# A deformable convolution that gathers a pixel with three differences: one multiply-add and one scaling a tap, two summing transposes

## The chip, the cores and the metric

The kernel runs on one core of a Trainium2 chip. The metric is the device time of one execution in microseconds (us). Engines are named as the profile names them: PE is TensorE (PEld its weight loads), DVE is VectorE, ACT is ScalarE, POOL is GpSimd, SP is SyncE, whose queue issues most DMAs. All data are 32-bit floats.

## What is computed

Two layers of a "metaformer" over x of shape (4, 128, 128, 128): four images, 128 channels, 128 rows, 128 columns. The part that matters here is the token mixer of layer 0, a deformable 3x3 convolution on the channel-normalised image. An ordinary 3x3 convolution gives 18 offsets a pixel, a (dy, dx) for each of nine taps. Each tap reads the image at its shifted, fractional place, as a weighted sum of the four pixels around it, and the nine samples are multiplied by nine 128x128 matrices and summed:

```python
offset = _offset_conv(x, w_off)                      # 18 channels
py = base_y + dy ; px = base_x + dx                  # of 9 taps
y0 = jnp.floor(py); x0 = jnp.floor(px)
wy1 = py - y0; wy0 = 1.0 - wy1
wx1 = px - x0; wx0 = 1.0 - wx1
sampled = (corner(y0, x0, wy0 * wx0) + corner(y0, x1, wy0 * wx1)
         + corner(y1, x0, wy1 * wx0) + corner(y1, x1, wy1 * wx1))
return jnp.einsum('bckhw,ock->bohw', sampled, w_conv.reshape(O, C, K * K))
```

A corner outside the image counts as zero. Behind the mixer come a mixture of eight experts for each token, a second mixer (an FFT pair that reduces to a channel product with a mirrored image) and a layer of 64 experts for selected tokens.

## The kernel before, in words

**Stages.** For each image a *table* is built in device memory (`tabs`, class `Image`, line 260): the normalised image with a border, where an entry (i, j) holds the 128 channels of the pixels (i-1, j-1) and (i, j-1), 1 KB; rows have `TC` = 130 entries. Two entries next to each other are the four corners of a sample, so a gather reads 2 KB at index `ylo * TC + xlo`. The image's `index` and `weight` tiles hold that index and the four products wy * wx for each pixel and tap. The first image's table is built ahead of the main loop, those of images 1 to 3 inside it, while the image before is sampled. The last image's period also holds the middle part of the 64 experts for images 0 to 2; a tail after the loop does the rest.

**Building a table.** `table_of` starts a `block` (line 507) for each 8 image rows. Its two halves (`half`, line 527) transpose four rows each to pixels by channels (`tr`), copy them to `raw`, compute mean and variance on VectorE, and write the normalised rows into `ent`. One DMA a block writes each row twice, as the lower pixel of one entry row and the upper one of the next; `ent[:, 0]` is a copy of the last row of the block before (`tails`). `padding` and `offsets` turn the same rows into the offset convolution, and `positions` with `axis_of` (lines 623 and 597) turn offsets into indices and weights for 16 rows.

**The main loop.** 4 images x 32 groups of four rows x 4 rows x 3 chunks of three taps: 1536 chunks of class `Chunk` (line 731), one to a *slot*. What is done for a chunk:

- `gather` (737): three indirect DMAs on POOL fill the chunk's buffer `g` [128 pixels, 3 taps, 4 corners, 128 channels]. There are `AHEAD` = 7 buffers; the gather for chunk n+7 is issued at the end of slot n and waits for chunk n's buffer.
- `weighted` (750), one slot before the sum: VectorE multiplies the corners by their weights, in one instruction for three taps (128x1536) if it is the first chunk of its row, and for two taps (128x1024) else. The weights come from `spread`, a tile in PSUM that `Group.weights` (693) fills by ScalarE copies. For the other chunks `weighted_too` (758) lets ScalarE scale the third tap, corner by corner.
- `summed` (766): TensorE transposes the four corners of each tap to channels by pixels, all into the same place of a PSUM bank `trg`, which adds them up: 12 transposes.
- `moved` (780), two slots later: ScalarE copies `trg` to `sT`. After each fourth chunk `convolved` multiplies by the tap matrices into the PSUM tile `sums`, and after the ninth tap `mixed` carries the group through the rest of the layer (experts `pe`, mirrored mixer, gate).

**What sets the order.** Engines run their instructions strictly in program order (`InOrder`), and waits are semaphores that the framework places. The order is written by hand: in each slot the loop at the end calls the steps of the chunks in flight, then `turns.steps()` resumes the jobs (generators) of the other work. A job that yields `FILL` waits until PSUM banks are to be had: `fills` (147) counts the banks taken in the last two slots against `BANKS` = 6. `turns.hop` is 1 before the main loop and 2 in it.

Of the kernel before, what the change touches and what calls it, by code (L numbers as in the profile page):

```python
# [51 lines left out]
P = 128  # L52
# [5 lines left out]
HID = 512  # L58
# [12 lines left out]
TC = P + 2  # L71
# [11 lines left out]
BANKS = 6  # L83
# [103 lines left out]
def metaformer_kernel(  # L187
# [50 lines left out]
    with ExitStack() as main:  # L238
# [19 lines left out]
        spread = p_s.tile([P, 2, 4, 4 * TAPS], F32, name="spread")  # L258

        class Image:  # L260


            def __init__(self, b):
                self.b = b
                self.table = tabs.tile([TW * TC, 2 * P], F32, name=f"table{b}", tag="table")
                self.grid = self.table.rearrange("(i j) e -> i j e", j=TC)
# [8 lines left out]
                self.offsets = self.placed = self.known = 0  # L275
# [4 lines left out]
            def room(self, q):  # L280
                return pw.tile(
                    [P, CB, TAPS, 4],
                    F32,
                    name=f"weight{self.b}_{q}",
                    tag="weight",
                    bufs=3 * P // CB // 2,
                )
# [7 lines left out]
            def border(self):  # L295

                eng.sync.dma_start(
                    out=self.grid[0:P, 0 : TC : TC - 1, :],
                    in_=zeros.unsqueeze(1).to_broadcast([P, 2, 2 * P]),
                )  # L300
                eng.sync.dma_start(
                    out=self.grid[P:TW, 0 : TC : TC - 1, :],
                    in_=zeros[0:1].unsqueeze(1).to_broadcast([1, 2, 2 * P]),
                )
# [46 lines left out]
        for base in (0, -P):  # L351
# [6 lines left out]
                pattern=[[1, P]],  # L358
                channel_multiplier=1,
# [75 lines left out]
        def padding(t, h, row, read, padded):  # L435

            yield FILL
            tr = transposes(row, 4)
            read.append(h)
            yield turns.hop  # L440
            eng.scalar.copy(pads[(2 * t + h) % 4][:, :, 1 : P + 1], tr)
            padded.append(h)

        def offsets(im, t, padded):
# [8 lines left out]
            for k in range(3):  # L453
                for h in range(2):
# [6 lines left out]
                    )  # L461
            yield turns.hop
# [31 lines left out]
        def again(im, t):  # L494
# [4 lines left out]
                in_=im.grid[t * RB : (t + 1) * RB, 1 : P + 1, P : 2 * P].rearrange("i x c -> x i c"),  # L499
# [3 lines left out]
            for h in range(2):  # L503
                turns.start(padding(t, h, lambda i, h=h: xc[:, 4 * h + i, :], [], padded))
            yield from offsets(im, t, padded)

        def block(im, t):

            while im.continued < t - 1 or im.sent < t - 1 or im.read < 2 * t:
                yield 1  # L510
            last = t == P // RB

            ent = pa.tile([P, RB + 1, P], F32, name=f"ent{im.b}_{t}", tag="ent")
            if t == 0:
                eng.vector.memset(ent[:, 0, :], 0.0)
            if last:
                eng.vector.memset(ent[:, 1, :], 0.0)
            else:
# [5 lines left out]
            im.tails[t] = ent[:, RB, :]  # L524
            halves, padded = [], []

            def half(h):
                yield FILL
                tr = transposes(lambda i: xc[:, 4 * h + i, :], 4)
                im.read += 1  # L530
                yield turns.hop
                raw = pa.tile([P, 4, P], F32, name="raw", tag="raw")
# [9 lines left out]
                yield 1  # L542
                if turns.hop == 1:

                    r, nb = rn
                    for i in range(1, 4, 2):
                        eng.vector.tensor_scalar(
                            ent[:, 1 + 4 * h + i, :],
# [7 lines left out]
                    normalise(  # L556
                        lambda i: raw[:, 2 * i, :], lambda i: ent[:, 1 + 4 * h + 2 * i, :], 2, even
                    )
                else:
                    normalise(  # L560
                        lambda i: raw[:, i, :], lambda i: ent[:, 1 + 4 * h + i, :], 4, rn
                    )
                yield 1
                if t < im.direct:
                    yield from padding(t, h, lambda i: ent[:, 1 + 4 * h + i, :], halves, padded)
                else:
                    halves.append(h)
# [8 lines left out]
            while im.normed < t:  # L576
                yield 1
            if t > 0:
                eng.scalar.copy(ent[:, 0, :], im.tails.pop(t - 1))
                im.continued = t  # L580
            while not last and len(halves) < 2:
                yield 1
            im.normed = t + 1
            n = 1 if last else RB
            i0 = t * RB
            yield 1
            pairs = ent[:, 0:2, :].rearrange("p i c -> p (i c)").unsqueeze(1)
            pairs = bass.AP(
                pairs.tensor, pairs.offset, [pairs.ap[0], [P, n], [1, 2 * P]]
            )  # L590
            eng.sync.dma_start(
                out=im.grid[i0 : i0 + n, 1 : P + 1, :].rearrange("i x e -> x i e"), in_=pairs
            )
            im.sent = t + 1
            im.left -= 1

        def axis_of(pos, which):
# [5 lines left out]
            w = pt.tile([P, 2, CB, TAPS], F32, name=f"w{which}", tag=f"w{which}")  # L603
# [13 lines left out]
            eng.vector.tensor_tensor(w[:, 1], pos, lo, ALU.subtract)  # L617
            yield 0
            eng.vector.tensor_scalar(w[:, 0], w[:, 1], -1.0, 1.0, ALU.mult, ALU.add)
            yield 1  # L620
            return lo, w

        def positions(im, q):
# [21 lines left out]
            ylo, wy = yield from axis_of(py, "y")  # L645
            xlo, wx = yield from axis_of(px, "x")
            eng.vector.scalar_tensor_tensor(xlo, ylo, float(TC), xlo, ALU.mult, ALU.add)
            yield 0
            eng.vector.tensor_copy(im.index[:, rows, :], xlo)
            im.weight[q] = im.rooms.pop(q, None) or im.room(q)  # L650
# [1061 lines left out]
```

## Time and profile before

| | before |
|---|---|
| median of 3 runs | 7367.58 us (7365.69 to 7368.79) |
| the profiled execution: its time / its span | 7358.05 us / 7356.1 us |
| mean granted TensorE clock | 0.896 |
| first gather / last gather issued at | 135.3 / 7123.6 us |
| first / last copy of `trg` to `sT` starts at | 146.5 / 7141.5 us |
| DMA queues, share of 16 engines' span: gathers q0, others q1 | 55.0% + 12.1% |
| moved by DMA | 1524.69 MB, 207 GB/s |

A page of the profile gives busy times of each engine, and then groups of like instructions: line, engine, operation, out<-in by tile names, count, then busy time and mean duration of one in ns, then idle time of the engine just before them and what ended most of it. "remote" is a semaphore event that the profile can't put down to an instruction, and "issue" is time in which the engine waited for nothing shown. All instructions that the wrapper `InOrder` issues have line 101, so groups are told apart by tile names. In a timeline the columns are start in us, duration in us, engine, operation, tiles, and in brackets the idle time before.

By image, the main loop's busy time a chunk is 3.75 to 3.81 us on PE, 2.93 to 3.04 on DVE, 2.19 to 2.38 on ACT and 2.85 to 2.86 on POOL, of 4.52 to 4.63 us.

### The profile page before, as it was taken

How to read it: one execution, taken by the hardware profiler on the slowest of the kernel's cores; microseconds unless marked ns; L12 is line 12 of the kernel's file. 1: busy time of each engine (PE TensorE's matmuls, PEld its weight loads, DVE VectorE, ACT ScalarE, POOL GpSimd, SP SyncE). 2: the span in 40 equal slices, each digit the busy share in tenths (PEclk: the TensorE clock that was granted, in tenths of full speed). 3: DMA queues.
4: the chain of work that ended last, by engine and by line, in shares of the span. 5: the costliest groups of instructions: out<-in, count | busy, mean ns of one | idle time of the engine just before them, and what ended most of it. 6: DMA issues, size and time to landing. Idle time of an engine off the chain costs nothing. (4 is left out here: it accounts for less than half of the span.)

```text
span 7356.1 us, 103037 instructions
## 1 busy us (share of the span) xinstructions
PE 6006.3 (82%) x31271; PEld 3981.9 (54%) x31271; DVE 4789.5 (65%) x16100; ACT 3707.7 (50%) x9999; POOL 4432.3 (60%) x4691
## 2 busy tenths in 40 slices
PE   5788888887888888887888888888877788788885
PEld 3455555555555555555555555555555555555553
DVE  5466666676667666666667666667667665566663
ACT  4345555554555555554455555555444444444452
POOL 1666666666666666666666666666666665666641
PEclk7888999998898998998899999898898999899897
DMA  6666666666666666666666666666666677677777
GB/s 204 191 200 212 204 207 210 202 194 188 197 201 203 205 206 200 204 193 186 193 209 200 207 202 201 198 199 210 186 189 181 201 250 238 180 247 237 246 236 273
DMA packets 578917, 1524.69 MB, mean 207 GB/s; under 512 B 86424, under 2 KB 225408, under 8 KB 578368
## 3 DMA queue, kind: packets, MB, share of 16 engines
q0 software_dynamic: 369664, 1210.35, 55.0%
q1 hardware_dynamic: 206400, 299.36, 12.1%
q10 hardware_dynamic: 2304, 8.39, 0.3%
q8 instruction: 254, 4.16, 0.2%
q14 instruction: 295, 2.42, 0.1%
HBM read 1380.92 MB, written 136.85 MB: 206 GB/s over the span
## 5 line engine op out<-in xcount | busy, mean ns | idle before, releaser
L101 POOL DMA_INDIRECT g<-table,index x4608 | 4377.4, 950 | 2710.4 <-issue 1190.9
L101 PEld LDWEIGHTS trg<-ident,g 128*128 128x128 f32 x18432 | 2300.2, 150 | 1501.3 <-issue 1288.2
L101 PE MATMUL trg<-ident,g 128*128 128x128 f32 x18432 | 2575.2, 288 | 562.9 <-issue 465.9
L101 DVE SCALAR_TENSOR_TENSOR x<-pe,scaled,x 128x128 f32<-128x128 f32 x4048 | 1379.7, 341 | 1432.5 <-remote 644.6
L101 DVE TENSOR_TENSOR g<-g,spread 128x1024 f32<-128x1024 f32 (+1 forms) x1536 | 2129.1, 1387 | 202.4 <-DMA g<-table,index 90.0
L101 ACT COPY sT<-trg 128x384 f32<-128x384 f32 x1536 | 720.5, 472 | 2742.1 <-remote 1187.4
L101 PE MATMUL sums<-sT,wconv_sb 128*128 128x512 f32 x2304 | 1326.6, 658 | 53.1 <-issue 50.9
L101 ACT ACTIVATE g<-g,weight 128x128 f32<-128x128 f32 x4096 | 1306.3, 394 | 1.9 <-DMA g<-table,index 1.7
L101 PE MATMUL pe<-ew_sb,x1T 128*128 128x512 f32 x2048 | 1163.6, 649 | 147.0 <-issue 88.6
L101 PEld LDWEIGHTS sums<-sT,wconv_sb 128*128 128x128 f32 x2304 | 435.1, 208 | 518.9 <-issue 516.5
L101 PEld LDWEIGHTS pe<-ew_sb,x1T 128*128 128x128 f32 x2048 | 343.7, 205 | 261.1 <-issue 182.3
L101 ACT ACT_TABLE_LOAD x270 | 346.4, 1283 | 23.5 <-DVE nmax L101 9.8
L101 PE MATMUL sums<-xg,ident 128*128 128x512 f32 x256 | 163.8, 726 | 125.8 <-ACT x1T L101 96.8
L101 DVE TENSOR_TENSOR x<-ps,x 128x512 f32<-128x512 f32 x128 | 88.1, 688 | 264.5 <-remote 119.6
L101 PE MATMUL po<-pad,woff_sb 128*64 128x512 f32 x768 | 216.1, 645 | 17.8 <-issue 11.0
L101 DVE TENSOR_TENSOR x<-x,pe 128x512 f32<-128x512 f32 x128 | 87.0, 679 | 217.8 <-remote 130.4
L101 PE MATMUL pl<-rw_sb,x1T 128*128 128x8 f32 x1024 | 143.9, 256 | 98.2 <-issue 88.7
L101 ACT ACTIVATE tn<-x,d_nb,d_rs 128x128 f32<-128x128 f32 x512 | 211.2, 487 | 5.5 <-DVE x L101 2.6
L101 ACT ACTIVATE xn<-x,c_nb,c_rs 128x128 f32<-128x128 f32 x512 | 210.6, 485 | 4.7 <-issue 1.8
L101 PEld LDWEIGHTS pl<-rw_sb,x1T 128*128 128x128 f32 x1024 | 147.3, 213 | 98.5 <-issue 88.6
L101 ACT ACTIVATE ent<-raw,a_nb,a_rs 128x128 f32<-128x128 f32 x448 | 185.0, 485 | 7.6 <-remote 3.8
L101 PE MATMUL pe<-eb_sb,gT 32*128 32x512 f32 x256 | 169.4, 740 | 20.0 <-issue 14.6
(227 smaller groups left out, 5130.9 us busy)
## 6 DMA issues: line engine op xcount, KB each, us to landing
g<-table,index POOLq DMA_INDIRECT x4608
table<-ent SPq DMA_DIRECT2D x64, 1024.0 KB
xc<-in_x SPq DMA_DIRECT2D x64, 512.0 KB
w<-x_d SPq DMA_DIRECT2D x64, 512.0 KB
xg<-in_x SPq DMA_DIRECT2D x124, 256.0 KB
x_d<-x SPq DMA_DIRECT2D x124, 256.0 KB
out<-w SPq DMA_DIRECT2D x48, 512.0 KB
w<-in_weight SPq DMA_DIRECT2D x40, 512.0 KB
```

The source lines that it names most:

```text
L101: return self.tc.keep_in_program_order(issue(*args, **kwargs))
```

## The change

An entry of the table grows from 1 KB to 2 KB and becomes a pixel with three differences, so that one entry holds all that a sample needs. With A the pixel above left, the sample is (A + wy * B) + wx * (C + wy * D), where B is the step downwards, C the step sideways and D the step downwards of C. An entry is laid out [A, C, B, D].

- The table: `TC` goes, rows have `TW` = 129 entries of 4 x 128 floats. A half block (`STEP` = 4 rows) is stored by itself. The step sideways is a matmul with the matrix `step` (-1 on the diagonal, +1 beside it; it mixes partitions, which are pixels) into a PSUM bank `beside`, copied by ScalarE; the step downwards is one subtraction of 128x1024 a half block, on GpSimd ahead of the main loop and on VectorE in it, after a copy of the last row of the half block before. The left border of each row gets its entries by small DMAs (`edge`), one more for each row of the image. `ent` has three buffers.
- Positions: the weights kept are wy and wx alone, computed straight into `weight`; the complements and the four products go, as do `spread` and `Group.weights`. `BANKS` becomes 7.
- The chunk: `down` (VectorE, three multiply-adds of 128x256, both tensors in SBUF, the weight a pointer to a column in SBUF) two slots before the sum; `beside` (ScalarE, three scalings of 128x128) one slot before; `summed` does two transposes a tap instead of four. The loop starts one slot earlier for it.
- Buffers of the 64 experts' weights move: one of `OWN` = 9 tiles of the end is made from two halves in two pools.

The core of the diff:

```diff
-                self.table = tabs.tile([TW * TC, 2 * P], F32, name=f"table{b}", tag="table")
-                self.grid = self.table.rearrange("(i j) e -> i j e", j=TC)
+                self.table = tabs.tile([TW * TW, 4 * P], F32, name=f"table{b}", tag="table")
+                self.grid = self.table.rearrange("(i j) e -> i j e", j=TW)
...
+                yield FILL
+                beside = bank([P, STEP, P], "beside")
+                eng.tensor.matmul(beside, lhsT=step, rhs=new[0], start=True, stop=True)
+                yield turns.hop
+                eng.scalar.copy(new[1], beside)
...
+                free = eng.gpsimd if turns.hop == 1 else eng.vector
+                if u == 0:
+                    free.memset(ent[:, 0:2, :], 0.0)
+                else:
+                    free.tensor_copy(ent[:, 0:2, :], im.tails.pop(u - 1))
...
+                free.tensor_tensor(
+                    of[:, :, half_of:], here[:, :, half_of:], of[:, :, 0:half_of], ALU.subtract
+                )
+                yield 1
+                stored(u, ent, STEP)
...
+            def stored(u, ent, n):
+
+                i0 = u * STEP
+                eng.sync.dma_start(
+                    out=im.grid[i0 : i0 + n, 1 : P + 1, :].rearrange("i x e -> x i e"),
+                    in_=ent[:, 0 : 4 * n].rearrange("p (i s) c -> p i (s c)", s=4),
+                )
+                for i in range(n):
+                    eng.sync.dma_start(
+                        out=im.edge(i0 + i, 1, 1),
+                        in_=ent[0:1, 4 * i : 4 * i + 4 : 2, :],
+                    )
+                im.sent = u + 1
...
-            for s in range(4):
-                if s % 2 == 0:
-                    yield 1
-                eng.vector.tensor_tensor(
-                    im.weight[q][:, :, :, s], wy[:, s % 2], wx[:, s // 2], ALU.mult
-                )
...
-            def weighted(self):
-                n = 2 if self.shared else 3
-                gf = self.g[:, 0:n].rearrange("p k s c -> p (k s) c")
-                w = self.row.group.w[:, self.row.s, 4 * self.k0 : 4 * (self.k0 + n)]
-                eng.vector.tensor_tensor(
-                    gf, gf, w.unsqueeze(2).to_broadcast(list(gf.shape)), ALU.mult
-                )
...
+            def down(self):
+
+                for i in range(3):
+                    eng.vector.scalar_tensor_tensor(
+                        self.g[:, i, 0:2, :],
+                        self.g[:, i, 2:4, :],
+                        self.weight(i, 0),
+                        self.g[:, i, 0:2, :],
+                        ALU.mult,
+                        ALU.add,
+                    )
+
+            def beside(self):
+
+                for i in range(3):
                     eng.scalar.activation(
-                        g[:, v, :], g[:, v, :], AF.Copy, scale=w[:, y % CB, self.k0 + 2, v : v + 1]
+                        self.g[:, i, 1, :], self.g[:, i, 1, :], AF.Copy, scale=self.weight(i, 1)
                     )
...
-                    for v in range(4):
+                    for v in range(2):
...
-            if n + 1 < total:
-                chunk[n + 1].weighted()
+            if n + 2 < total:
+                chunk[n + 2].down()
...
-            if n >= 0 and n + 3 < total and (n + 3) % 12 == 0:
-                chunk[n + 3].row.group.weights((n + 3) // 12 % 2)
-            if n + 1 < total and chunk[n + 1].shared:
-                chunk[n + 1].weighted_too()
+            if 0 <= n + 1 < total:
+                chunk[n + 1].beside()
```

## The prediction

> **What bounds the kernel now.** I read the page's busy shares first, then the tile `trg` with those who wait for it, then the costliest groups, and last GpSimd's timeline.
>
> ```profile
> PE 6006.3 (82%) x31271; PEld 3981.9 (54%) x31271; DVE 4789.5 (65%) x16100; ACT 3707.7 (50%) x9999; POOL 4432.3 (60%) x4691
> ```
>
> TensorE is the busiest. The view of tile `trg`, the PSUM tile of the summing transposes, says who stands behind it:
>
> ```profile
> L101 ACT COPY sT<-trg x1536: 452/479/509, 146.5 to 7141.5; 128x384 f32<-128x384 f32 x192
> ...
> who waited for it (us, times):
>   ACT sT L101: 597.7, 204
>   POOL g L101: 501.1, 250
>   DVE x L101: 321.0, 107
> ```
>
> Three things: the loop over 1536 chunks (three taps of one image row) runs from 146.5 to 7141.5 us, 6995 us or 4.554 us a chunk; 146.5 us lie before it and 214.6 behind. ScalarE, VectorE and GpSimd wait for these transposes, so TensorE sets the pace. And GpSimd's wait is for buffers, not for work. How far behind it stands is told by a stretch in which its buffers are free, and one in which they run out:
>
> ```profile
> 166.78 0.94 POOL L101 DMA_INDIRECT g<-table,index  x1 [0.30 <-issue]
> 168.03 0.95 POOL L101 DMA_INDIRECT g<-table,index  x1 [0.30 <-issue]
> 173.64 0.95 POOL L101 DMA_INDIRECT g<-table,index  x1 [4.66 <-remote]
> 174.89 0.95 POOL L101 DMA_INDIRECT g<-table,index  x1 [0.30 <-issue]
> ```
>
> Free-running gathers start 1.25 us apart (0.95 of work, 0.30 of issue; from 149.24 to 168.03 there are 15 steps in 18.79 us, 1.253 each). A chunk has three: 3.758 us. The loop therefore has a second floor at 1536 x 3.758 = 5772 us, and the difference of 0.797 us a chunk is what GpSimd now waits.
>
> **The change, part by part.**
>
> ```profile
> L101 PE MATMUL trg<-ident,g 128*128 128x128 f32 x18432 | 2575.2, 288 | 562.9 <-issue 465.9 <-ACT sT L101 33.6 <-DVE g L101 26.9
> L101 PE MATMUL sums<-sT,wconv_sb 128*128 128x512 f32 x2304 | 1326.6, 658 | 53.1 <-issue 50.9 <-ACT sT L101 0.2
> L101 DVE SCALAR_TENSOR_TENSOR x<-pe,scaled,x 128x128 f32<-128x128 f32 x4048 | 1379.7, 341 | 1432.5 <-remote 644.6 <-PE pe L101 293.8 <-PE trg L101 263.8
> L101 ACT ACTIVATE g<-g,weight 128x128 f32<-128x128 f32 x4096 | 1306.3, 394 | 1.9 <-DMA g<-table,index 1.7
> L101 DVE TENSOR_TENSOR g<-g,spread 128x1024 f32<-128x1024 f32 x1024 | 1237.9, 1209 | 171.1 <-ACT spread L101 81.2 <-DMA g<-table,index 63.0 <-issue 12.9
> L101 DVE TENSOR_TENSOR g<-g,spread 128x1536 f32<-128x1536 f32 x512 | 891.3, 1742 | 31.4 <-DMA g<-table,index 27.0 <-issue 2.5 <-PE trg L101 1.9
> ```
>
> *TensorE.* Half of 18432 transposes go: 9216 x 2575.2/18432 = 0.1397 us, 1288 us or 0.838 a chunk, on the pacing path. The new `beside` matmul (128 of them, two passes each like every f32 matmul here) costs 2 x 1326.6/2304 = 1.15 us; 96 fall into the loop: 111 us, 0.072 a chunk. If every other TensorE time and wait stays, the pace is 4.554 - 0.838 + 0.072 = 3.788. A TensorE with less to do may be granted less clock: it had 0.92 in 500 to 1500 us, where it was busy 853 of 1000, and 0.75 at the end, where it was busy 118 of 206. Its busy time would fall from 3.76 to 3.00 a chunk; at 0.80 instead of 0.90 that is 3.38, still under the floor of GpSimd. No charge.
>
> *VectorE.* Out: 2129 us of products, 128 weight products of 0.423 (54), 64 small scalings (15). In: 4608 multiply-adds of 128x256. No such row exists. Below: the two products give 143 ns plus 1.041 an element, 409 ns. Above: the 128x128 multiply-add with a pointer took 341 where that line gives 276, so 65 more, 474. I take 442, the middle: 2037 us. 96 subtractions of 128x1024 at 1.209 and 93 copies of 128x256, at most 0.41 each: 154 us at most. Net about zero, 3.1 us a chunk, under both floors.
>
> *ScalarE.* 512 more scalings at 1306.3/4096 = 0.319 (163), 128 evacuations of `beside` at 0.584 (75, the row of the `raw` copy); 272 copies of spread weights (53) and 64 tail copies (20) go. 165 us more, 2.5 us a chunk: hidden behind GpSimd's 3.76; uncovered it would cost 0.11 a chunk.
>
> *Gathers.* As many, of 2 KB as before. The buffer is needed one slot earlier (`down` at n+2), five slots after it came free instead of six: five slots of 4 us against three issues and a landing. The DMA queues were busy 67% of the span; at 4.07 a chunk that is 75%, and the doubled table (68 MB more on 1525) makes it 78%. No charge.
>
> *A new hold-up.* `spread`, the second operand of the old products, lies in PSUM; both tensor operands of the new multiply-adds lie in SBUF. The trace has a few such instructions in the loop, and they delay gathers:
>
> ```profile
> 251.69 0.44 DVE L101 TENSOR_TENSOR off<-z 128x288 f32<-128x288 f32 x1
> 251.84 1.11 POOL L101 DMA_INDIRECT g<-table,index  x1 [0.30 <-issue]
> ...
> 253.07 0.46 DVE L101 TENSOR_TENSOR off<-off,z 128x288 f32<-128x288 f32 x1 [0.74 <-issue]
> 253.25 1.10 POOL L101 DMA_INDIRECT g<-table,index  x1 [0.30 <-issue]
> ...
> 5655.28 0.69 DVE L101 TENSOR_TENSOR same<-same,val 128x512 f32<-128x512 f32 x1
> 5655.37 1.42 POOL L101 DMA_INDIRECT g<-table,index  x1 [0.30 <-issue]
> ```
>
> Each gather that began inside such an instruction is longer by that instruction's remaining time less about 0.13 us: at 251.84, 0.29 remained and it took 0.16 more; at 5655.37, 0.60 and 0.47. The products with `spread`, in flight during 2533 gathers, leave them at 0.95. With 442 ns a hit costs on average (0.442 - 0.13)^2/(2 x 0.442) = 0.11, with a second one overlapping its end some 0.15; three in 3.9 us are hit by about a third of the gathers: 0.047 a gather, 0.14 a chunk (bounds: nothing; and 0.31 a gather if every one begins just after a multiply-add). The 96 subtractions add 0.01. GpSimd's pace becomes 3.91.
>
> The Trainium skill, "SBUF — State Buffer", section "Who interferes with whom", says that a VectorE instruction with two SBUF inputs and a GpSimd instruction that reads SBUF exclude each other, the later one blocked until the earlier has finished. The trace agrees for the gathers, but not the other way: `off` instructions that began 190 to 770 ns into a gather took 0.44 to 0.47, like the others. By the rule each gather would need 0.95 + 0.30 + 0.44 = 1.69 us, and the total would be about 8,200; an estimate that I set aside for the rows.
>
> *Before the loop.* The first image's table is built before any gather. GpSimd now subtracts there: 456 ns at 128x128 and 725 at 128x256 (its own additions near the end) extend to 2.34 us at 128x1024, with a copy about 3 us, 32 times: 96 us of some 120. The table writes double to 34 MB; the queues were 63% busy in these 135 us. SyncE issues four small edge DMAs more per half block, 0.5 us each by the row of the border's small DMAs. All are under the stage's time but several near it: +20 us (bounds 0 and 45). Behind the loop nothing that counts moves.
>
> *Sum.* The two paces, 3.79 and 3.91, are now so close that each waits for the other. Of the 0.797 that GpSimd waits I leave a fifth, 0.16 (bounds 0 and two fifths): a choice. 4.07 x 1536 = 6252; with 166.5 before and 214.6 behind, 6633. The profiled execution took 7358.05 for a span of 7356.1, 2 more; the median of the runs, 7367.58, is 0.13% over it: 6640.
>
> **The rivals.**
>
> *GpSimd's floor alone* (0.14): few hits, buffers swallow the rest; 3.80 a chunk, 5837 + 381 = 6220. For it: seven chunks of gathers ahead. Against: the shown hold-ups.
>
> *VectorE becomes the pace* (0.13): in program order the multiply-adds wait for gathers, and the sums of the experts `x<-pe` stand behind them. Its 3.1 us plus the 1.13 a chunk for which `x<-pe` now waits (894.7 remote, 389.8 `pe`, 310.4 `trg`, 147.2 `tr`) are 4.25: 6530 + 381 = 6910. Against: that wait is for TensorE, which has less to do.
>
> *Every gather meets a multiply-add* (0.15, slower): if VectorE runs dry, each multiply-add starts when its own gather lands, at a fixed point of GpSimd's rhythm; where that is just ahead of the next gather's start, all pay 0.31: 4608 x 1.565 = 7211 + 381 = 7590. It decides from 0.26 a gather, where the loop takes its present 6995. Against: the phase would have to hold, and VectorE is busy three quarters of the time.
>
> *The transposes were not what paces* (0.03): about 7360. For it: TensorE idles 1350 us, much of it for nothing shown.
>
> **How the numbers follow.** My forecast, 6350 to 6900, has 0.52 plus 0.03 at its edges, 0.55. The range 6200 to 7150 holds it, most of the first rival and the second; its top is 0.10 a gather of hold-up with two fifths of the wait, 4.38 x 1536 + 395 = 7123. Faster 0.55 + 0.14 + 0.13 = 0.82; within 0.2%, about what a measurement of this kernel can tell from no change, 0.03; slower 0.15.
>
> **What would show it.** Gathers with a mean near 1.00 instead of 0.95, their idle time nearly all 0.30 of issue; `trg` 9216 times near 0.14; multiply-adds between 0.41 and 0.47; first `sT` near 166; TensorE busy 72%, at a lower clock. I am wrong if gathers last 1.2 us or more, if VectorE's multiply-adds show waits for gathers as its largest idle time, or if TensorE's busy time falls and its idle time takes the same amount.

## The result, and the profile after

| | before | after |
|---|---|---|
| median | 7367.58 us (7363.04 to 7370.72, 5 runs) | 7407.54 us (7401.98 to 7412.89, 5 runs) |
| after / before | | 1.0054, 95% interval 1.0040 to 1.0069 |
| span of the profiled execution | 7356.1 us | 7405.5 us |
| first gather | 135.3 us | 203.3 us |
| main loop, first to last start of `sT` | 6995.0 us | 6975.1 us |
| mean granted TensorE clock | 0.896 | 0.830 |

Half a per cent slower, where 6640 us were forecast. Three parts of the changed kernel's profile answer to those shown of before. First the page's busy times:

```profile
PE 5353.5 (72%) x22311; PEld 3087.4 (42%) x22311; DVE 4756.0 (64%) x19171; ACT 3855.4 (52%) x10304; POOL 4706.9 (64%) x4758
```

Then the tile `trg`, with the same rows as before:

```profile
L101 ACT COPY sT<-trg x1536: 449/473/512, 218.3 to 7193.4; 128x384 f32<-128x384 f32 x192
...
  POOL g L101: 458.6, 272
...
  ACT sT L101: 436.5, 160
```

And the costliest groups (busy time, mean ns | idle time just before and what ended it):

```profile
L101 POOL DMA_INDIRECT g<-table,index x4608 | 4563.0, 990 | 2389.2 <-issue 1193.1 <-ACT sT L101 301.3 <-remote 282.0
L101 DVE SCALAR_TENSOR_TENSOR g<-g,weight 128x256 f32<-128x256 f32 x4608 | 1973.5, 476 | 382.8 <-DMA g<-table,index 258.1 <-issue 106.1 <-remote 5.1
...
L101 PE MATMUL trg<-ident,g 128*128 128x128 f32 x9216 | 1519.4, 304 | 831.5 <-issue 253.1 <-remote 205.6 <-ACT g L101 140.5
...
L101 DVE SCALAR_TENSOR_TENSOR x<-pe,scaled,x 128x128 f32<-128x128 f32 x4048 | 1375.8, 340 | 1275.0 <-remote 666.8 <-PE trg L101 147.7 <-PE pe L101 129.2
...
L101 ACT COPY sT<-trg 128x384 f32<-128x384 f32 x1536 | 722.4, 470 | 2133.3 <-remote 1086.8 <-PE trg L101 432.7 <-PE pe L101 167.7
```

Two of these rows in the kernel before:

```profile
L101 POOL DMA_INDIRECT g<-table,index x4608 | 4377.4, 950 | 2710.4 <-issue 1190.9 <-ACT sT L101 367.7 <-remote 326.3
...
L101 ACT COPY sT<-trg 128x384 f32<-128x384 f32 x1536 | 720.5, 472 | 2742.1 <-remote 1187.4 <-PE trg L101 597.7 <-PE pe L101 555.4
```

TensorE's busy time fell by 653 us and its idle time took them: the loop still needs 4.541 us a chunk (4.554 before). The start lost 72 us, the loop won 20 and the end 2.5: these are the 49 us between the two spans (the medians are 40 apart). No engine is busy for three quarters of the loop. What stands out is the word "remote": on one core no other core can be meant, yet ScalarE's copies waited 1087 us for an event that the profile can't put down to an instruction, and so did VectorE's `x` (909 us over all its forms). One such place in the timeline of the changed kernel, GpSimd's, ScalarE's, VectorE's and TensorE's lines together (start, duration, and in brackets the idle time before):

```profile
3093.67 2.80 PE L101 MATMUL po<-pad,woff_sb 128*64 128x512 f32 x12
...
3101.64 0.95 POOL L101 DMA_INDIRECT g<-table,index  x1 [0.30 <-issue]
...
3102.59 1.02 PE L101 MATMUL sums<-sT,wconv_sb 128*128 128x512 f32 x2
...
3108.02 0.95 POOL L101 DMA_INDIRECT g<-table,index  x1 [0.30 <-issue]
3109.27 0.95 POOL L101 DMA_INDIRECT g<-table,index  x1 [0.30 <-issue]
3113.51 0.59 ACT L101 COPY os<-po 128x512 f32<-128x512 f32 x1 [11.94 <-remote]
3113.65 0.35 DVE L101 SCALAR_TENSOR_TENSOR x<-pe,scaled,x 128x128 f32<-128x128 f32 x1 [8.86 <-remote]
```

The convolution `po` ended at 3096.5; ScalarE's copy of it starts at 3113.5. The trace's events of TensorE's semaphore show why: none between 3094.4 and 3113.5, and then six in 0.31 us, too many to have been worked off in that time. TensorE was done, its completions came late, all at once, and only after GpSimd had run out of buffers and stopped issuing gathers at 3110.2. This is how it mostly goes. Counted over the loop by the time since the last gather began:

| time since the last gather began | share of the time | TensorE's semaphore events per us |
|---|---|---|
| before, 0 to 1.25 us (gathers run back to back) | 82% | 0.36 |
| before, 2.25 to 4 us (GpSimd waits) | 8% | 5.0 |
| after, 0 to 1.25 us | 82% | 0.57 |
| after, 2.25 to 4 us | 7% | 6.9 |

It is no strict rule: 59% of the events before and 56% after come more than 1.25 us after a gather began, in 18% of the time, and more than half of the others during the first three gathers after a pause. The trace also lacks some events (of the 9561 that the changed kernel's TensorE makes it has 7686), but if all of those had come while gathers ran back to back, the rate there would be 0.9 and not 0.57, far from 6.9.

In the kernel before, ScalarE stood idle ahead of 730 of its 1536 copies of `trg`, and they began a median of 5.0 us after their last transpose had ended in the records. I had read these waits as TensorE's work. The other engines' completions were not late: where ScalarE or VectorE stood idle for the other (`c_rs` after `c_mv` and back), it began a median of 0.03 to 0.04 us after the other had ended, and TensorE 0.05 us after ScalarE's `x1T`, in both traces.

### The profile page after: what moved, and what is told of

Same layout as the page of the kernel before. It is cut to its first block, busy times and chain, and to the rows that moved or that the text cites. A ratio compares the mean times of both kernels' runs of the same rounds, so it can differ in the third digit from the quotient of the medians.

```text
span 7405.5 us, 90159 instructions
## 1 busy us (share of the span) xinstructions
PE 5353.5 (72%) x22311; PEld 3087.4 (42%) x22311; DVE 4756.0 (64%) x19171; ACT 3855.4 (52%) x10304; POOL 4706.9 (64%) x4758
## 4 chain that ended last, share of the span: by engine, by line
PE 41%; DVE 18%; another core or an unknown queue 15%; issue 11%; ACT 6%; DMA 4%; POOL 3%; SPq 0%; POOLq 0%; ACTq 0%; DVEq 0%
PE sums L101 10%; PE pe L101 10%; PE trg L101 10%; DVE x L101 5%; DVE g L101 5%; PE tr L101 3%; POOL g L101 3%; DMA g<-table,index 3%; PE po L101 2%; ACT g L101 2%; PE pl L101 1%; PE beside L101 1%; PE pq L101 1%; ACT sT L101 1%
## 5 line engine op out<-in xcount | busy, mean ns | idle before, releaser
L101 POOL DMA_INDIRECT g<-table,index x4608 | 4563.0, 990 | 2389.2 <-issue 1193.1
L101 DVE SCALAR_TENSOR_TENSOR g<-g,weight 128x256 f32<-128x256 f32 x4608 | 1973.5, 476 | 382.8 <-DMA g<-table,index 258.1
L101 PE MATMUL trg<-ident,g 128*128 128x128 f32 x9216 | 1519.4, 304 | 831.5 <-issue 253.1
L101 PEld LDWEIGHTS trg<-ident,g 128*128 128x128 f32 x9216 | 1253.2, 158 | 1822.2 <-issue 947.5
L101 ACT ACTIVATE g<-g,weight 128x128 f32<-128x128 f32 x4608 | 1520.1, 396 | 67.4 <-DVE g L101 35.1
L101 PE MATMUL sums<-sT,wconv_sb 128*128 128x512 f32 x2304 | 1411.7, 698 | 107.9 <-ACT sT L101 53.8
L101 PE MATMUL pe<-ew_sb,x1T 128*128 128x512 f32 x2048 | 1231.7, 686 | 292.8 <-issue 155.6
L101 PEld LDWEIGHTS sums<-xg,ident 128*128 128x128 f32 x256 | 52.5, 246 | 393.7 <-ACT x1T L101 286.7
L101 PE MATMUL beside<-ent,step 128*128 128x512 f32 x256 | 167.2, 744 | 65.8 <-remote 27.2
L101 DVE BATCH_NORM_STATS2 a_st<-raw 128x6 f32<-128x128 f32 x512 | 136.1, 277 | 72.0 <-ACT raw L101 55.0
```

What stands on the lines that cost most here:

```text
L101: return self.tc.keep_in_program_order(issue(*args, **kwargs))
```

## The experiments

The theories: A, TensorE's work paces the loop and the relief was given back elsewhere. B, TensorE's completions come through only in pauses of the gathers, and the loop is the gathers and the pauses that the hand-overs need. C (on the second kind of chip GpSimd's issuing of gathers alone is the pace) and D (on the first kind a gather takes some 1.5 us on the average, and that is the pace) came out of the runs. Each group of runs met another chip, and the chips turned out to be of two kinds: the kernel before took 7279.8 to 7365.8 us on three of them, called the first kind here (the chip of the profiles above is like them), and 6165.5 and 6167.9 us on two, the second kind. No chip was met twice, so that a kind could also be a state that a chip was in at the time. The kernel before has no profile on the second kind; e1 stands in for it there.

| run | kind of chip | us | to before on its chip | loop, us a gather | TensorE busy, us |
|---|---|---|---|---|---|
| changed kernel (r1) | first | 7405.64 | 1.0055 | 1.513 | 5306 |
| before, one transpose a tap (e7) | first | 7210.19 | 0.9906 | 1.487 | 4791 |
| after, no multiply-adds (e5) | first | 7350.73 | 0.9980 | 1.502 | 5284 |
| before, 64-byte gathers (e9) | first | 7246.81 | 0.9958 | 1.495 | 5990 |
| before, pauses on GpSimd (e10) | first | 7291.46 | 1.0017 | 1.503 | 6033 |
| before, results used one slot later, not two (e12) | first | 7332.22 | 0.9958 | 1.515 | 5935 |
| after, few experts (e13) | first | 7375.64 | 1.0016 | 1.516 | 4861 |
| the same, three slots later (e14) | first | 7400.87 | 1.0052 | 1.507 | 4916 |
| after, copy and subtraction on VectorE (e6) | first | 7388.75 | 1.0031 | 1.514 | 5315 |
| the same, fewer border DMAs (e11) | first | 7350.71 | 0.9980 | 1.507 | 5340 |
| before, no gathers (e8) | first | 5382.58 | 0.7395 | none | 5210 |
| before, two transposes a tap (e1) | second | 6163.90 | 0.9997 | 1.260 | 4869 |
| changed kernel (r2) | second | 6469.94 | 1.0489 | 1.310 | 5075 |
| after, four transposes a tap (e2) | second | 6466.34 | 1.0487 | 1.309 | 5686 |
| after, 64-byte gathers (e4) | second | 6508.37 | 1.0555 | 1.319 | 5115 |
| before, spaced gathers (e16) | second | 6860.23 | 1.1123 | 1.411 | 5708 |
| before, four gathers a chunk (e15) | second | 8082.61 | 1.3104 | 1.257 | 6134 |
| after, no gathers (e3) | second | 5166.30 | 0.8379 | none | 4630 |

The fifth column is the loop, from the first to the last start of `sT`, over the number of gathers: 4608, or 6144 in e15.

**Transposes alone: e1 and e2, second kind; e7, first kind.**

```diff
# e1: before
-                    for v in range(4):
+                    for v in range(2):
-                            stop=(v == 3),
+                            stop=(v == 1),
# e2: after, the reverse of it
# e7: before, range(1) and stop=True
```

> The kernel before with two summing transposes a tap instead of four and nothing else changed: the corners 2 and 3 of every sample are left out. Theory A (the prediction's: TensorE's work paces the loop, the relief is real, and the new version gives it back through what else it does): 9216 transposes of 0.1397 us fall away, 1288 us, down to GpSimd's own 3.76 to 3.9 us a chunk; 6150 to 6450 us. Theory B (what TensorE finishes reaches ScalarE, VectorE and GpSimd only in the pauses of GpSimd's back-to-back gathers; the loop is the gathers plus the pauses that the hand-overs need, whatever TensorE has to do): 7250 to 7420 us.

> The changed kernel with four transposes a tap again (it also adds the steps B and D, which the sample does not want): TensorE's relief is undone inside the new version. Theory A: 1288 us or more come on top, 8300 to 8700 us. Theory B: TensorE's work is not what paces, 7380 to 7600 us.

> The kernel before with a single transpose a tap (three of four corners are left out): 13824 transposes less, 1931 us of TensorE's work. Theory A: the loop falls to GpSimd's pace, 6150 to 6350 us. Theory B, on a chip where the kernel before takes 7366 us (TensorE's completions held while GpSimd issues gathers): 7280 to 7380 us. On a chip where it takes 6165 us, theory C: 6150 to 6175 us.

e1 took 6163.90 us; it lies in A's window only because the kernel before, on that chip, takes 6165.5 itself: ratio 0.9997 (0.9988 to 1.0007). 1288 us of transposes less bring nothing, and 9216 more in e2 cost nothing against the changed kernel (6466.34 and 6469.94 us). On the first kind e7 takes three quarters of the transposes away for 0.9% (0.9906, 0.9888 to 0.9924), below B's window but far from A's. Neither kind of chip is paced by them. Nor is TensorE's clock what parts the two kinds: e1 was granted 0.904, the kernel before 0.896 on the first kind. The rows of e1 and then e7 show the two kinds:

```profile
L101 POOL DMA_INDIRECT g<-table,index x4608 | 4366.9, 948 | 1534.4 <-issue 844.7 <-DMA g<-table,index 171.8 <-DMA xg<-in_x 131.0
...
L101 ACT COPY sT<-trg 128x384 f32<-128x384 f32 x1536 | 702.0, 462 | 163.1 <-PE trg L101 162.0
```

```profile
L101 POOL DMA_INDIRECT g<-table,index x4608 | 4379.0, 950 | 2563.2 <-issue 1218.4 <-ACT sT L101 332.8 <-remote 196.8
...
L101 PE MATMUL trg<-ident,g 128*128 128x128 f32 x4608 | 913.9, 311 | 790.0 <-issue 353.0 <-ACT sT L101 135.6 <-ACT g L101 65.2
L101 ACT COPY sT<-trg 128x384 f32<-128x384 f32 x1536 | 715.1, 470 | 1666.2 <-remote 1072.5 <-PE trg L101 267.6 <-issue 100.9
```

In e1 no copy waits for "remote" at all, a copy that did wait began 0.037 us after its transpose, and the gathers follow one another with hardly a pause, 1.260 us each: GpSimd's own 0.95 and 0.30. In e7, with even fewer transposes, the copies still wait 1073 us for "remote".

**Without gathers: e3 (after) and e8 (before). Small gathers: e4 (after) and e9 (before).**

```diff
# e3, e8
-                    eng.gpsimd.indirect_dma_start(...)
+                    eng.sync.dma_start(out=self.g[:, i]..., in_=neighbouring entries)
# e4, e9
-                        out=self.g[:, i].rearrange("p s c -> p (s c)"),
+                        out=self.g[:, i, 0, 0:16],
```

> The changed kernel with each gather replaced by a plain DMA of the same 128 x 2 KB, of neighbouring entries instead of the indexed ones, issued by SyncE: GpSimd has nothing to do in the loop, the bytes moved stay. Theory A: GpSimd was not the bound, so at most the hold-ups go: 7250 to 7400 us. Theory B, if it is GpSimd's issuing of gathers that holds TensorE's completions back: ScalarE's and VectorE's waits for nothing shown shrink to a fraction of their 1087 and 909 us, and the loop falls to what TensorE's 3.3 and VectorE's 3.0 us a chunk allow, 3.5 to 4.1: 5800 to 6700 us. Theory B, if it is the traffic of the gathers: no change.

> The kernel before with plain DMAs of SyncE in place of the gathers (as many bytes, of neighbouring entries instead of the indexed ones). TensorE has 3.75 to 3.81 us a chunk to do. Theory B, if GpSimd's issuing of gathers holds TensorE's completions: the waits for nothing shown go, and TensorE itself becomes the pace, 3.8 to 4.1 a chunk, 6150 to 6600 us, on either kind of chip. Theory B, if it is the traffic, or theory A on the chip where the kernel before takes 7366 us: 7200 to 7400 us.

> The changed kernel with gathers of 64 bytes a pixel instead of 2 KB (a 32nd of the bytes, as many gathers, by the same indices; the rest of each buffer holds what was there). Theory B, if it is the issuing of gathers that holds TensorE's completions back: 7300 to 7420 us, the waits for nothing shown as before. Theory B, if it is the traffic: the loop falls to 3.8 to 4.0 us a chunk, GpSimd's own pace, 6200 to 6600 us. Theory A: 7300 to 7420 us too.

> The kernel before with gathers of 64 bytes a pixel instead of 2 KB, as many of them, by the same indices; the rest of each buffer holds what was there. Where the kernel before takes 7366 us: theory B by the issuing 7250 to 7420 us with ScalarE's sT waiting 900 us or more for nothing shown; theory B by the traffic 6150 to 6600 us with hardly any such wait. Where it takes 6165 us: 6150 to 6200 us.

e3 fell below its window, to 5166.30 us, and e8, on the first kind, to 5382.58. The busy times, the loop and the copies' waits of e8:

```profile
PE 5209.5 (97%) x31271; PEld 3635.2 (68%) x31271; DVE 4752.5 (88%) x16100; ACT 3727.6 (69%) x9999; POOL 54.9 (1%) x83
```

```profile
L101 ACT COPY sT<-trg x1536: 452/479/497, 140.1 to 5166.0; 128x384 f32<-128x384 f32 x192
```

```profile
L101 ACT COPY sT<-trg 128x384 f32<-128x384 f32 x1536 | 721.8, 471 | 1027.4 <-PE trg L101 1010.4 <-issue 10.5 <-PE pq L101 5.2
```

This is a loop that TensorE paces: 3.27 us a chunk, 97% busy, with all the kernel's transposes in it. It beat the 3.75 us that I had taken for TensorE's need, for the most part since its clock was 0.985 instead of 0.896 (that alone would make it 3.41). And the lateness is gone: on the chip on which e7's copies, where they waited, began a median of 4.9 us after their last transpose, those of e8 began 0.037 us after it, and none waited for "remote". The chip alone does not make TensorE's completions late; the gathers on it do. So before's 4.55 was 1.28 above what TensorE needs. What the gathers cost is not their traffic: e9 moves a 32nd of it for 0.4% (0.9958, 0.9942 to 0.9975), 4.49 us a chunk, and e4 gains nothing on r2. One part of e9's expectation failed: its copies wait for "remote" 478 us, not 900; 1195 us are now put down to `trg`, while TensorE's events are still far denser in the pauses (some 14 a us there, 1.1 during gathers). The label moved, the pattern did not.

**VectorE's part, and the changed kernel again: r1 and e5.**

```diff
# e5: after
-            if n + 2 < total:
-                chunk[n + 2].down()
```

> The changed kernel itself, beside the kernel before on the same chip, since the first four runs came from a chip on which the kernel before takes 6165 us. Theory C (where TensorE's completions come through at once, the loop of both kernels runs at the pace at which GpSimd issues gathers, so the change can only cost: hold-ups of gathers by the multiply-adds, and the slower start): 3758 ns a chunk before, 3900 to 3960 after, and 72 us before the loop: 6440 to 6480 us, 1.045 to 1.051 of before. Theory A: 5500 to 6000 us. On a chip like that of the first profile: 1.004 to 1.007 of before.

> The changed kernel without its multiply-adds (the rows of pixels below are left out of the samples). Theory C: with nothing on VectorE that meets the gathers but the small rest, gathers last 0.95 us again, the loop returns to 3.76 to 3.79 a chunk; 6190 to 6260 us where the kernel before takes 6165, and all that stays of the loss is the start. If the loss came from the chain through VectorE, ScalarE and TensorE or from the subtractions: 6350 us or more. On a chip like that of the first profile: 7250 to 7420 us.

r1 repeats the result on another chip of the first kind (1.0055, 1.0038 to 1.0072). e5 takes the 1974 us of multiply-adds from VectorE, and gathers last 0.959 us again; the loop is 52 us shorter than r1's 6971.9. On this kind, then, VectorE doesn't pace the loop either, and the hold-ups of gathers hardly count. What they cost without pauses to hide them r2 shows:

> The changed kernel once more, on whatever chip these runs meet: 1.004 to 1.007 of before where the kernel before takes 7280 to 7370 us; 1.045 to 1.055 where it takes 6165 us.

6469.94 us, 1.0489 (1.0472 to 1.0507): the change costs nine times as much there, in per cent. From r2's groups and from its timeline:

```profile
L101 POOL DMA_INDIRECT g<-table,index x4608 | 4606.9, 1000 | 1411.5 <-issue 897.0 <-DMA g<-table,index 167.0 <-PE trg L101 82.6
L101 DVE SCALAR_TENSOR_TENSOR g<-g,weight 128x256 f32<-128x256 f32 x4608 | 2102.4, 480 | 1409.1 <-DMA g<-table,index 1370.9 <-PE trg L101 4.1 <-PE sums L101 2.3
```

```profile
3003.31 0.48 DVE L101 SCALAR_TENSOR_TENSOR g<-g,weight 128x256 f32<-128x256 f32 x1 [0.91 <-DMA g<-table,index]
3003.53 1.08 POOL L101 DMA_INDIRECT g<-table,index  x1 [0.30 <-issue]
```

A gather that begins 0.26 us before the end of a multiply-add takes 1.08 instead of 0.95. The mean gather is 1.000 us against e1's 0.948; each of 4608 takes 0.051 more of the loop (1.310 against 1.260), 234 us; the start takes 72 more; the difference of the medians is 302. VectorE's largest wait is now for gathers. TensorE's events come evenly there: 1.5 a us during gathers and 1.6 in the few pauses, by the same program whose rates in the table above are 0.57 and 6.9.

**Pauses and distances: e10, e12, e13, e14.** Theory B gave the 4.5 us a reading: what TensorE finishes is used two slots later, so one pause of 1.5 us in two chunks.

```diff
# e10: before
+                if self.row.s % 2:
+                    pause = pb.tile([P, 512], F32, name="pause", tag="junk", bufs=1)
+                    eng.gpsimd.memset(pause, 0.0)
+                    eng.gpsimd.memset(pause[:, 0:256], 0.0)
# e12: before; hop stays 1 in the loop
-                chunk[n - 2].moved()
+                chunk[n - 1].moved()
# e13: after
-AHEAD = 7
+AHEAD = 6
-                for n in range(9):
+                for n in range(3):
# e14: e13 with
-        turns.hop = 2
+        turns.hop = 3
-                chunk[n - 2].moved()
+                chunk[n - 3].moved()
```

> The kernel before with two memsets of 1.56 us together put among GpSimd's gathers after every second chunk. Theory B says why the loop takes 4.52 us a chunk: what TensorE finishes is used two slots later, so that GpSimd has to pause for 1.5 us once in two chunks, (6 x 1.253 + 1.5) / 2 = 4.51; a pause put there takes the place of the one that came of itself: where the kernel before takes 7366 us, 4.5 to 4.75 a chunk, 7300 to 7700 us. If the pauses add to what sets the loop: 5.3 a chunk and more, over 8400 us. Where it takes 6165 us the work of GpSimd simply grows: 4.55 to 4.75 a chunk, 7350 to 7650 us.

> The kernel before with what TensorE finishes used one slot later instead of two, in the main loop, the copy of trg too. Theory B: a pause of GpSimd's gathers is then needed in every chunk, 3 x 1.253 + 1.5 = 5.26 us a chunk where the kernel before takes 7280 to 7370 us: 8200 to 8700 us. Where it takes 6165 us: the gathers go on setting the pace, 3.76 to 4.0 a chunk, 6150 to 6550 us. Had the gathers no part in it, the two chips would lose alike.

> The base for the next run: the changed kernel with three quarters of the expert products and their sums left out, six gather buffers for seven and one buffer more for x1 and x1T. A quarter to a third less work on TensorE and VectorE. Theory B, where the kernel before takes 7280 to 7370 us: the loop stays near 4.4 to 4.55 us a chunk, 7150 to 7430 us. Where it takes 6165 us: 3.85 to 3.95, 6380 to 6480 us.

> The kernel of e13 with what TensorE finishes used three slots later instead of two (the sum of the taps alone stays at two). Theory B: one pause of GpSimd in three chunks instead of two, 1.5/2 - 1.5/3 = 0.25 us a chunk less than e13, some 380 us: 6750 to 7050 us where the kernel before takes 7280 to 7370 us. Where it takes 6165 us: as e13, within 60 us. Without theory B a longer way through the slots gains nothing: as e13 on both.

e10's groups:

```profile
L101 POOL DMA_INDIRECT g<-table,index x4608 | 4383.9, 951 | 1939.0 <-issue 1284.3 <-ACT sT L101 140.6 <-DMA xg<-in_x 131.0
...
L101 ACT COPY sT<-trg 128x384 f32<-128x384 f32 x1536 | 723.4, 473 | 2678.4 <-remote 987.1 <-PE trg L101 620.1 <-PE pe L101 507.5
...
L101 POOL MEMSET pause<- 128x512 f32 (+1 forms) x1536 | 658.5, 429 | 44.4
```

The two memsets came to 0.91 us together, not to the 1.56 that the expectation counts on, and e10's chip is the faster one of the first kind (7279.8 against 7366 us), so that this is a smaller test than was meant. Still, 659 us of memsets among the gathers are taken up by the pauses that came of themselves (GpSimd's idle time ahead of gathers fell from 2710 to 1939 us) and cost 0.17% (0.07 to 0.28). That fits B, and D as well. But the loops of e12 and e14 throw its formula out:

```profile
L101 ACT COPY sT<-trg x1536: 451/478/512, 145.9 to 7127.0; 128x384 f32<-128x384 f32 x192
```

```profile
L101 ACT COPY sT<-trg x1536: 452/464/502, 221.5 to 7163.9; 128x384 f32<-128x384 f32 x192
```

With one slot the loop takes 4.545 us a chunk (e12; 5.26 expected), with three 4.520 (e14; 0.25 less than e13's 4.548 expected, so 4.30). The runs of gathers only change their length: on the average 6.3 gathers between pauses of 1.97 us in e12, 10.0 and 2.50 in e13, 11.4 and 2.65 in e14, 5.0 and 1.54 in e10 (from the end of one gather to the start of the next, where that is over 0.4 us). What stays is the sum, and that is theory D: on the first kind a gather takes 1.49 to 1.52 us on the average, 1.25 of them issuing, in whatever rhythm. All these kernels have three gathers a chunk, so they can't tell a pace of 1.5 us a gather from one of 4.5 us a chunk.

**Each gather by itself: e15, e16.**

```diff
# e15: before
-                for i in range(3):
-                    k = self.k0 + i
+                for i in range(4):
+                    k = self.k0 + i % 3
# e16: before, after each gather
+                    eng.gpsimd.memset(pause, 0.0)
```

> The kernel before with a fourth gather in each chunk (the first tap's once more, never read) and five buffers of four taps for seven of three. e12 and e14 have thrown out the distance of the hand-overs. Theory D: on the chips where the kernel before takes 7280 to 7370 us a gather takes 1.50 to 1.52 us on the average, in whatever rhythm, and that alone sets the loop: 6144 x 1.51 + 360, 9500 to 9750 us. If 4.5 us is a limit of the chunk and not of the gather: 4 x 1.253 = 5.01 a chunk, 8050 to 8250 us. Where the kernel before takes 6165 us: 8050 to 8250 us.

> The kernel before with a memset of 128x192 after every gather, which spaces the gathers about 1.55 us apart. Theory D, on the chips where the kernel before takes 7280 to 7370 us: gathers that come no faster than one in 1.51 us leave no backlog, so TensorE's completions come at once, the waits for nothing shown (ScalarE's sT 1187 us, VectorE's x 645 us) nearly vanish, and the time is that of the spaced gathers, 4.55 to 4.8 a chunk, 7350 to 7750 us. If every gather holds TensorE's completions back by itself, backlog or not: the waits stay over 600 us, and the time is above 7800 us.

Both met a chip of the second kind, so that D was not put to this test. There e15 takes 8082.61 us, 1.257 us a gather, as expected; e16's memsets spaced the gathers by 0.16 us, less than meant, and the loop takes 1.411 us a gather. Both confirm only that GpSimd's issuing is the whole pace on that kind.

**The start: e6 and e11.**

```diff
# e6: after
-                free = eng.gpsimd if turns.hop == 1 else eng.vector
+                free = eng.vector
# e11: e6, and
-                for i in range(n):
-                    eng.sync.dma_start(out=im.edge(i0 + i, 1, 1), in_=ent[0:1, ...])
+                eng.sync.dma_start(out=im.edge(i0, n, 1).unsqueeze(0), in_=ent[0:1, ...])
```

> The changed kernel with the copy and the subtraction of each half block on VectorE ahead of the loop too, not on GpSimd. If GpSimd's 3 us a half block, 32 times, are what delays the first gather from 135 to 203 us: the first gather near 150, 45 to 60 us less than the changed kernel. If the doubled stores and the small DMAs of the left border delay it: less than 15 us less.

> The changed kernel with the copy and the subtraction of a half block on VectorE ahead of the loop, as in e6, and one DMA for the left border's entries of a half block in place of four. If SyncE's queue (ten issues, 7.4 us, in some 9.5 us of a block in e6) is what the start still waits for: the first gather from 181 to 160 us or less, the time 20 us or more below e6, 1.000 of before or less where the kernel before takes 7280 to 7370 us. If the doubled stores or the longer chain of a half block set the start: the first gather at 173 us or more, 1.002 to 1.004.

The first gather is issued at 202.6 us in r1, at 181.5 in e6 and at 178.0 in e11. e6 falls between the two windows of its expectation: GpSimd's copy and subtraction are 21 of the 67 us that the first gather lost, the border's small DMAs 3.5. The other 43 lie with the doubled stores or the longer chain of a half block; these two were not told apart. e11's time, 7350.71 us, is 0.998 of before (0.9970 to 0.9989): the only complete version of the changed kernel below the kernel before, by 0.2%, on the first kind; its loop is 26 us shorter than r1's, which the start does not explain. e12, a complete version of the kernel before, gains more there by using results one slot sooner: 0.9958 (0.9942 to 0.9974). On the second kind neither was run.

## Why the prediction was wrong

*What bounds the kernel now* is the step that failed: "ScalarE, VectorE and GpSimd wait for these transposes, so TensorE sets the pace". They waited for completions of TensorE that came late, for the most part in pauses of the gathers. The row of `x<-pe` that the prediction shows has "remote 644.6" as its largest releaser, and the rival that counts it says "that wait is for TensorE, which has less to do", without a look at when TensorE's work had ended. e1, e2 and e7 show that the transposes do not pace; e8 shows what TensorE's pace is, 3.27.

*TensorE.* The sizes were near (1288 us off and 111 on forecast; busy 3.3 us a chunk in the loop, 3.00 to 3.38 forecast), and the lower clock came: 0.83, with transposes of 0.165 us for 0.140, so that their row fell by 1056 us. But "if every other TensorE time and wait stays" did not hold: the waits grew by what the work lost, the clause under which I had called myself wrong. That the sign "TensorE busy 72%" came true is luck: both the busy time and the whole time came out higher than forecast, in nearly the same proportion.

*Gathers.* "The loop therefore has a second floor at 1536 x 3.758" is right on the second kind alone, where the kernel before runs on it. On the first kind a gather takes 1.49 to 1.52 us of the loop in eleven kernels with 4791 to 6033 us of TensorE's work, with and without VectorE's multiply-adds, with a 32nd of the traffic. So "the difference of 0.797 us a chunk is what GpSimd now waits" was no reserve to be won.

*The new hold-up* was right in mechanism and size: 0.047 us a gather forecast, 0.040 measured on the first kind (990 against 950 ns), 0.052 on the second. GpSimd's pace of 3.91 a chunk is what the second kind shows (3.93). e5 shows whose it is: without the multiply-adds a gather takes 959 ns. On the first kind most of it vanishes in pauses that come anyway: in e5 the gathers take some 145 us less than in r1, the loop 52.

The Trainium skill, "SBUF — State Buffer", section "Who interferes with whom", was rightly set aside as a price: by the estimate made from its rule a gather would need 1.69 us, and r2 shows 1.310. The gathers do wait as it says; the multiply-adds do not: those of the changed kernel that began within a gather took 474 ns and the others 479. The same section says that TensorE and ScalarE never wait on anyone; that their results are seen at once does not follow, as the first kind shows.

*VectorE.* 476 ns a multiply-add, just above the bound of 474; 442 was taken. VectorE is not the pace on either kind; the rival in which it is adds 3.1 and 1.13 to 4.25, where they make 4.23, and its work in the loop came to 2.96 us a chunk. *ScalarE*: 3855 us busy, 148 more than before, 165 forecast, hidden. *Interplay*, 0.16 a chunk "a choice": on the second kind 0.02.

*Before the loop* was mis-sized: 72 us for 20, over the upper bound of 45. GpSimd's 3 us a half block explain 21 of them (e6), and the border's DMAs 3.5 (e11).

Of the rivals the one held least likely came true, "the transposes were not what paces", about 7360 us; the start's 72 us less the loop's 20 make up the rest to the 7407 measured, within some 5 us.

**What stays open** is what makes a gather take 1.5 us on the first kind, when GpSimd issues it in 1.25. Its data are not slower: by the traces' DMA packets they have landed a median of 3.4 us after the gather began, before and after, and 3.4 in e1 on the second kind. That TensorE's completions are the cause of the pauses, since they free the buffers that GpSimd waits for, or that both queue behind something which takes 1.5 us for each gather, was only argued; e16 was to tell, and met the wrong kind of chip; so did e15, which was to part the gather from the chunk. The small differences between first-kind loops (1.487 to 1.518 us a gather) have hardly a reading here either, but the three of e7, e9 and e10 come from the chip on which the kernel before takes 86 us less than on the others.

## What to carry to other kernels

Before an engine is taken for the pace, see whether those that wait for it start when its work ends: here they started 5 us later, and then its work is not what they wait for. A stage with the gathers taken out (e8) shows in one run what the busiest engine can do, and would have told it before any transpose was saved. Where one engine issues back to back (the second kind here), every term that touches that engine counts, and the relief of another counts for nothing. Where it pauses in a proportion that no other engine's work moves (the first kind), its own terms hardly counted either: 659 us of memsets on GpSimd cost 0.17%.

## What the runs showed of the hardware

- On chips of the first kind TensorE's completions reached other engines late while GpSimd issued gathers back to back: copies of `trg` that had to wait began a median of 5.0 us after their last transpose (before; 6.2 after, 4.9 in e7). Without gathers, on e7's chip, it was 0.037 us (e8), as on the two chips of the second kind with gathers (e1, r2). Between ScalarE and VectorE it was 0.03 to 0.04 us on the first kind too.
- The same kernel takes 7366 us on one chip and 6166 on another, and the same change costs 0.5% on one kind and 4.9% on the other: 1.0055 (1.0038 to 1.0072) against 1.0489 (1.0472 to 1.0507).
- The mean clock granted to TensorE went with its share of busy time in these runs, not strictly: 0.985 at 97% busy (e8), 0.896 at 82% (before), 0.920 at 81% (e12), 0.830 at 72% (after), 0.787 at 66% (e7).
- A multiply-add of 128x256 with both tensors in SBUF and a pointer takes 476 ns and lengthens a gather that begins within it by its remaining time less 0.13 us: with 0.25 to 0.30 us left gathers took 1.10 us instead of 0.95, with 0.35 to 0.40 left 1.19. Those that began in its first 0.03 us took 0.95. It is not itself lengthened (474 ns within a gather, 479 outside).
